# Order of four blocks in a unit of the third pass: image by image instead of column by column

## The chip, the cores and the metric

The kernel runs on one core of a Trainium2 chip. The metric is the time of one execution on the device in microseconds (us); before and after are compared by their medians over several runs. The profile is one traced execution.

## The reference: what is computed

The input x has the shape (8, 96, 96, 192), all float32. Two blocks follow each other, each of the form x + f(groupnorm(x)). The group norm has 32 groups of 6 channels, over a whole image.

The first block projects 192 channels to 384, convolves each channel by 3 x 3, runs four exponential moving averages (left, right, up and down), mixes them with the convolution, normalises over the 384 channels (layer norm) and projects back:

```python
mixed = 0.25 * (lr + rl + tb + bt) + local
mu = jnp.mean(mixed, axis=-1, keepdims=True)
var = jnp.mean(jnp.square(mixed - mu), axis=-1, keepdims=True)
normed = (mixed - mu) * jax.lax.rsqrt(var + LN_EPS) * ln_g + ln_b
return jnp.einsum('bhwc,cd->bhwd', normed, W_out) + b_out
```

The second block convolves each channel by 7 x 7, applies a layer norm, a product to 768 channels, a GELU, a product back to 192 channels and a scale per channel.

## The kernel before, in words

The kernel has five passes with DRAM arrays between them: group norm and projection (results in P_d), convolution and averages (M_d), **layer norm, projection back and the statistics of the second group norm (X1_d, X2_d)**, the 7 x 7 convolution (Y_d), and the two products with the GELU. The change lies in the third.

The third pass works through 192 **units**. A unit has two columns of pixels (WB = 2, counted by j) of two images (b = 0, 1). Every combination of column and image is a **block** of 96 pixels (S = 96, one image column) by 384 channels (C, three pieces of 128, NC = 3). The program of each engine is written out by hand, in the order of the calls (a manual schedule), so the order of the loops is the order of TensorE's queue.

- load_c(u) (lines 809 to 826) loads a unit: mt, the mixed values, 128 channels on the partitions, three transfers; and xr, the pixels of x, two transfers. It is called three units ahead; mt has four buffers.
- block_c (828 to 844) is one block. TensorE transposes the three pieces into the PSUM tile pt (L833), then multiplies them by the weights wc (L835). wc has 193 columns: 192 of the projection, and one of 1/384, so that column 192 of the result is the mean. ScalarE (ACT) copies this mean out of PSUM (L839), and then squares the transposed values minus the mean with a running sum (L842), which gives the variance.
- scale_c (846 to 851) makes 1/sqrt(variance) of the unit before, on DVE (L848) and POOL (L850).
- finish_c (853 to 874) reads the four results of the unit before from PSUM on DVE, scales them and adds xr (L858), stores them to X2_d (L867) and copies them to x1c (L871), from which store_c (L931) writes X1_d one part per unit.
- group_steps (876 to 926) are the statistics of the second group norm, spread over the units on DVE (L887, ten per unit), and at the end of each pair of images some longer steps, with small matmuls (L51, L52, L71, L911).

PSUM tiles of the results: each column has its own tile po of 128 x 2 x 193 floats, which holds both images beside each other, and there are four such tiles in all (two units). The lines that the prediction follows:

```python
831  lhs = [mt[:, m, WB - 1 - j, b, :] for m in range(NC)]
832  for m in range(NC):
833      nc.tensor.transpose(pt[:S, m * 128 : (m + 1) * 128], lhs[m], ident)
834  for m in range(NC):
835      nc.tensor.matmul(
836          po[:S, b], lhs[m], wc[:, m], start=(m == 0), stop=(m == NC - 1)
837      )
838  mean = sp.tile([S, 1], F32, tag="mean", name="mean", bufs=4)
839  nc.scalar.copy(mean, po[:S, b, D:])
...
842  nc.scalar.activation(
843      sq, pt[:S], AF.Square, bias=mean, scale=-1.0, accum_out=var[:, k : k + 1]
844  )
```

and the place that calls them, unit by unit, after the loads of three units ahead, a store, and scale_c of the unit before; the statistics' steps and finish_c of the unit before follow it:

```python
965  pos = [ps_o.tile([128, 2, D + 1], F32, tag="po", name="po") for _ in range(WB)]
966  for j in range(WB):
967      for b in range(2):
968          block_c(mt, pos[j], var, j, b)
```

The waits between engines come from the framework's tracking of tiles: a product into a po tile waits for the readers of that tile that stand before it in the program, whichever half they read.

Of the kernel before, what the change touches and what calls it, by code (L numbers as in the profile page):

```python
# [84 lines left out]
def conv_blocks_kernel(  # L85
# [137 lines left out]
    with ExitStack() as ph:  # L223
# [247 lines left out]
        with tc.manual_schedule():  # L471
# [13 lines left out]
            for b in range(B):  # L485
                more = b + 1 < B
                for t in range(n_t):
                    u = b * n_t + t

                    n, j = divmod(u - 2, NJ)  # L490
# [25 lines left out]
                    k, j = divmod(t, NJ)  # L516
# [181 lines left out]
    def load_weights():  # L698
        with nc.allow_non_contiguous_dma(reason="one value per partition"):
            for p, k, c in spans:  # L700
                nc.scalar.dma_start(w0w[p, k], w0[c])
                nc.scalar.dma_start(aff[p, k, 0:1], ln_gamma[c].unsqueeze(1))
                nc.scalar.dma_start(aff[p, k, 1:2], ln_beta[c].unsqueeze(1))
            nc.scalar.dma_start(b0g, b0.rearrange("(m p) -> p m", p=128))
        nc.scalar.dma_start(w1g, w1.rearrange("(m p) d -> p m d", p=128))
        nc.scalar.dma_start(lsc, gamma.partition_broadcast(128))
        nc.scalar.dma_start(b1g, b1.partition_broadcast(128))
# [19 lines left out]
    WB = 2  # L727
# [12 lines left out]
    def load_d(m):  # L740
        c = m * HC
        row = D * WV * B
        pool = d_pools[m % ND > 0]
        xin = pool.tile([128, NT, BP, HC, 2 * WV], F32, tag="xin", name="xin")

        for t in range(NT):
            for g, eng in enumerate((nc.sync, nc.gpsimd)):
                src = bass.AP(
                    tensor=X1_d.tensor,
                    offset=X1_d.offset + (2 * t + g) * HG * PH * row + c * WV * B,  # L750
                    ap=[[row, 64], [1, HC * WV * B]],
                )
                eng.dma_start(
                    xin[g * 64 : (g + 1) * 64, t].rearrange("q a c n -> q (a c n)"), src
                )
        band = pool.tile([128, HC, ZW], F32, tag="band", name="band1")
        for g, eng in enumerate((nc.sync, nc.gpsimd)):
            eng.dma_start(
                band[g * 64 : (g + 1) * 64].rearrange("q c l -> q (c l)"),
                Z2_d[:, c : c + HC].rearrange("r c l -> r (c l)"),  # L760
            )
        return band, xin
# [4 lines left out]
    with ExitStack() as ph:  # L767
# [41 lines left out]
        def load_c(u):  # L809

            k, v = divmod(u, n_c)
            bp, w = k // NH, v * WB * PH + k % NH
            we = w + (WB - 1) * PH + 1
            b = slice(2 * bp, 2 * bp + 2)
            mt = ip.tile([128, NC, WB, 2, S], F32, tag="mt", name="mt")
            for m in range(NC):
                nc.sync.dma_start(
                    mt[:, m].rearrange("c w b h -> c w (b h)"),
                    M_d[S - we : S - w : PH, m * 128 : (m + 1) * 128, b, :].rearrange(
                        "w c b h -> c w (b h)"  # L820
                    ),
                )
            xr = ip.tile([S, 2, WB, D], F32, tag="xr", name="xr", bufs=5)
            for i in range(2):
                nc.sync.dma_start(xr[:, i], x[2 * bp + i, :, w:we:PH, :])
            return mt, xr

        def block_c(mt, po, var, j, b):

            pt = ps_t.tile([128, C], F32, tag="pt", name="pt")  # L830
            lhs = [mt[:, m, WB - 1 - j, b, :] for m in range(NC)]
            for m in range(NC):
                nc.tensor.transpose(pt[:S, m * 128 : (m + 1) * 128], lhs[m], ident)  # L833
            for m in range(NC):
                nc.tensor.matmul(  # L835
                    po[:S, b], lhs[m], wc[:, m], start=(m == 0), stop=(m == NC - 1)
                )
            mean = sp.tile([S, 1], F32, tag="mean", name="mean", bufs=4)
            nc.scalar.copy(mean, po[:S, b, D:])  # L839
            sq = sp.tile([S, C], F32, tag="sq", name="sq", bufs=1)  # L840
            k = 2 * j + b
            nc.scalar.activation(  # L842
                sq, pt[:S], AF.Square, bias=mean, scale=-1.0, accum_out=var[:, k : k + 1]
            )

        def scale_c(var):
            ve = sp.tile([S, 2 * WB], F32, tag="ve", name="ve")
            nc.vector.tensor_scalar(ve, var, 1.0 / C, LN0_EPS * KAPPA**2, ALU.mult, ALU.add)  # L848
            rs = sp.tile([S, 2 * WB], F32, tag="rs", name="rs")
            nc.gpsimd.tensor_tensor(rs, ve, neg_half[:S, : 2 * WB], ALU.pow)  # L850
            return rs

        def finish_c(x1c, part, w, pos, rs, xr):
            x1u = sp.tile([S, WB, 2, D], F32, tag="x1u", name="x1u", bufs=3)
            for j in range(WB):
                for b in range(2):
                    k = 2 * j + b
                    nc.vector.scalar_tensor_tensor(  # L858
                        x1u[:, j, b],
                        pos[j][:S, b, :D],  # L860
                        rs[:, k : k + 1],
                        xr[:, b, j],
                        ALU.mult,
                        ALU.add,
                    )

            nc.gpsimd.dma_start(  # L867
                X2_d[part // NH, part % NH, :, w : w + WB].rearrange("h v b c -> h (v b c)"),
                x1u.rearrange("h v b c -> h (v b c)"),
            )  # L870
            nc.vector.tensor_copy(  # L871
                x1c[:, :, w : w + WB].rearrange("h c v b -> h (v b) c"),
                x1u.rearrange("h v b c -> h (v b) c"),
            )
# [53 lines left out]
        def store_c(x1c, k, q):  # L928
            c = slice(q * D // NX, (q + 1) * D // NX)
            bp, p = divmod(k, NH)  # L930
            nc.sync.dma_start(  # L931
                X1_d[p : S * PH : PH, c.start // HC : c.stop // HC, bp].rearrange(
                    "h g c v b -> h g (c v b)"
                ),
                x1c[:, c].rearrange("h (g c) v b -> h g (c v b)", c=HC),
            )
# [10 lines left out]
        with tc.manual_schedule():  # L947
            load_weights()
            for u in range(n_u + 1):
                if u + 3 < n_u:  # L950
                    ahead.append(load_c(u + 3))
                if stores:
                    stores.pop(0)()
                if held is not None:
                    rs = scale_c(held[1])
                if u < n_u:
                    mt, xr = ahead.pop(0)
                    nc.gpsimd.tensor_tensor(
                        xr.rearrange("p b w c -> p (b w) c"),
                        xr.rearrange("p b w c -> p (b w) c"),  # L960
                        cst.unsqueeze(1).to_broadcast([S, 2 * WB, D]),
                        ALU.add,
                    )
                    var = sp.tile([S, 2 * WB], F32, tag="var", name="var")
                    pos = [ps_o.tile([128, 2, D + 1], F32, tag="po", name="po") for _ in range(WB)]
                    for j in range(WB):
                        for b in range(2):
                            block_c(mt, pos[j], var, j, b)
                if steps:
                    for step in steps.pop(0):  # L970
                        step()
                if held is not None:
                    k, t = divmod(u - 1, n_c)
                    if t == 0:
                        x1c = xp.tile([S, D, WC, 2], F32, tag="x1c", name="x1c")
                    finish_c(x1c, k, t * WB, held[0], rs, held[2])
                    if (t + 1) % n_s == 0:
                        steps += group_steps(x1c, k, (t + 1) // n_s - 1)
                    if t == n_c - 1:
                        stores = [lambda q=q, x=x1c, k=k: store_c(x, k, q) for q in range(NX)]  # L980
                held = (pos, var, xr) if u < n_u else None

            stores.pop(0)()
            first_d = load_d(0)
            for store in stores:
                store()
            for step in sum(steps, []):
                step()
# [354 lines left out]
```

## Time and profile before

| what | value |
|---|---|
| median of three runs | 5908.91 us (5907.85 to 5926.22) |
| span of the profiled run | 5915.1 us |
| mean granted TensorE clock | 0.979 |
| TensorE busy | 5651.4 us, 96% |
| DVE, ACT, POOL busy | 3454.8, 2429.1, 2561.6 us |
| lines of block_c, first to last start | 1847.3 to 2928.5 us |
| products of the pass (L835) | 4608 records, 327 ns each (median) |
| copy of the mean (L839) | 768 times, 155 ns (median) |
| square with its sum (L842) | 768 times, 577 and 189 ns (median) |

How to read it: PE is TensorE's matmuls, PEld its weight loads, which run beside them. One float32 matmul stands as two records, so a block has six records of L835. A busy share is of the whole span; PE's busy time overlaps from one matmul to the next, so a PE at 100% can still be slowed by a wait. The releaser named at an idle time is the instruction that ended the wait.

### The profile page before, as it was taken

What the parts mean: (1) busy time and instruction counts of PE and PEld (TensorE: products, weight loads), DVE (VectorE), ACT (ScalarE), POOL (GpSimd) and SP (SyncE); (2) the same over time, 40 slices, a digit from 0 to 9 for tenths busy, and PEclk for the clock granted to TensorE, in tenths of its full rate; (3) what the DMA queues carried; (4) which work ended last, traced back from release to release, by engine and by line L of the source; (5) the groups of instructions that cost most, each with busy time, mean ns of one, the idle gap of its engine ahead of it and who ended that gap; (6) DMA issues with size and microseconds to landing.
All of it is one profiled execution on the core that took longest, in us unless ns stands there. A gap on an engine that the chain in (4) does not pass through costs nothing.

```text
span 5915.1 us, 122868 instructions
## 1 busy us (share of the span) xinstructions
PE 5651.4 (96%) x48550; PEld 3971.6 (67%) x48550; DVE 3454.8 (58%) x8023; ACT 2429.1 (41%) x6146; POOL 2561.6 (43%) x2731
## 2 busy tenths in 40 slices
PE   6999989999998999999878869999999999999999
PEld 3655533333335989898767757777777777777777
DVE  5555459999996667777733334444444444444443
ACT  2444447777775555555434322222222222222221
POOL 1111138888886666666522223323333333333332
PEclk9999989999999999999989989999999999999999
DMA  7999779999997889888899952232323232323221
GB/s 205 279 284 262 217 211 244 244 245 244 243 243 201 256 262 267 262 266 262 240 317 332 316 130 74 63 77 64 80 65 81 64 80 65 80 60 81 63 65 39
DMA packets 634283, 1054.49 MB, mean 178 GB/s; under 512 B 108683, under 2 KB 509284, under 8 KB 633708
## 3 DMA queue, kind: packets, MB, share of 16 engines
q1 hardware_dynamic: 516924, 620.81, 40.3%
q0 software_dynamic: 110656, 423.20, 22.0%
q8 instruction: 384, 6.29, 0.5%
q10 hardware_dynamic: 6128, 2.61, 0.2%
q14 instruction: 191, 1.56, 0.1%
HBM read 585.19 MB, written 476.72 MB: 180 GB/s over the span
## 4 chain that ended last, share of the span: by engine, by line
PE 78%; DMA 5%; issue 1%; DVE 1%; POOL 1%; SPq 0%; ACT 0%; ACTq 0%; POOLq 0%; DVEq 0%
PE po L1232 19%; PE po L835 14%; PE hp L1202 12%; PE pl L582 10%; PE hp L1212 7%; PE pa L603 5%; PE pt L833 4%; PE py L1030 3%; DMA xin<-X_d 3%; PE pa L606 2%; PE pt L1185 2%; DMA Y_d<-yo 2%; DMA X_d<-x1c 0%; DMA P_d<-po 0%; SPq L1067 0%
## 5 line engine op out<-in xcount | busy, mean ns | idle before, releaser
L1221 ACT ACTIVATE g<-hp,b0g 128x384 f32<-128x384 f32 x1152 | 564.4, 589 | 1830.5 <-PE hp L1212 1830.5
L1232 PE MATMUL po<-w1g,g 128*128 128x192 f32 x6912 | 1160.0, 327 | 0.0
L1232 PEld LDWEIGHTS po<-w1g,g 128*128 128x128 f32 x6912 | 1118.8, 190 | 1.1 <-issue 1.1
L835 PE MATMUL po<-wc,mt 128*96 128x193 f32 x4608 | 912.8, 333 | 0.0
L1189 DVE COPY yT<-pt 128x384 f32<-128x384 f32 x288 | 251.0, 871 | 1043.3 <-PE pt L1185 1043.1
L1202 PE MATMUL hp<-yT,w0w 128*128 128x384 f32 x2304 | 781.4, 489 | 0.4 <-DVE yT L1189 0.4
L835 PEld LDWEIGHTS po<-wc,mt 128*96 128x96 f32 x4608 | 701.8, 163 | 68.2 <-ACT mean L839 64.8
L1250 POOL DMA_DIRECT2D out_dram<-xo x576 | 342.9, 597 | 875.4 <-DVE xo L1239 860.6
L582 PE MATMUL pl<-pin,band 34*32 34x380 f32 (+1 forms) x13824 | 629.7, 489 | 18.5 <-DMA pin<-P_d 18.5
L1202 PEld LDWEIGHTS hp<-yT,w0w 128*128 128x128 f32 x2304 | 429.5, 191 | 257.2 <-issue 3.2
L612 DVE TENSOR_TENSOR_SCAN z<-decay,loc 128x768 f32<-128x768 f32 x288 | 505.9, 1757 | 60.1 <-ACT loc L591 30.7
L652 POOL TENSOR_TENSOR mo<-mo,z 128x768 f32<-128x768 f32 x288 | 530.1, 1841 | 3.4 <-ACT mo L607 0.4
L29 POOL TENSOR_TENSOR rs<-rs_ve,neg_half 96x8 f32<-96x8 f32 x96 | 159.2, 1659 | 824.1 <-DVE rs_ve L28 804.0
L582 PEld LDWEIGHTS pl<-pin,band 34*32 34x32 f32 x13824 | 232.7, 107 | 397.5 <-issue 396.2
L621 DVE TENSOR_TENSOR_SCAN z<-decay,z 128x768 f32<-128x768 f32 x288 | 498.3, 1730 | 0.0
L1030 PE MATMUL py<-xin,band 63*64 63x248 f32 (+1 forms) x6912 | 409.5, 392 | 74.7 <-DVE xin L1015 46.3
L842 ACT ACTIVATE sq<-pt,mean 96x384 f32<-96x384 f32 x768 | 443.5, 578 | 25.7 <-ACT mean L839 0.8
L1030 PEld LDWEIGHTS py<-xin,band 63*64 63x64 f32 x6912 | 354.4, 141 | 129.5 <-DVE xin L1015 36.5
L603 PE MATMUL pa<-loc,mix 128*32 128x384 f32 x3456 | 431.9, 493 | 0.0
L606 PE MATMUL pa<-last,down 96*32 96x384 f32 x1152 | 426.8, 493 | 1.0 <-ACT mo L607 1.0
L1212 PE MATMUL hp<-yT,w0w 64*128 64x384 f32 x2304 | 423.5, 500 | 0.0
L365 PE MATMUL pm<-xT,win 128*128 128x384 f32 x1152 | 395.8, 494 | 5.2 <-DVE po L389 5.2
(116 smaller groups left out, 7621.5 us busy)
## 6 DMA issues: line engine op xcount, KB each, us to landing
P_d<-po POOLq DMA_DIRECT2D x96, 1152.0 KB, 9.6
pin<-P_d SPq DMA_DIRECT2D x192, 576.0 KB
mt<-M_d SPq DMA_DIRECT2D x576, 192.0 KB
xq<-in_x_dram SPq DMA_DIRECT2D x96, 576.0 KB
xr<-in_x_dram SPq DMA_DIRECT2D x384, 144.0 KB
X_d<-x1u POOLq DMA_DIRECT2D x192, 288.0 KB, 4.2
X_d<-x1c SPq DMA_DIRECT2D x192, 288.0 KB
y<-Y_d SPq DMA_DIRECT2D x24, 2304.0 KB
```

The lines of the kernel that those rows point to most:

```text
L582: nc.tensor.matmul(pls[g][at * RB : (at + 1) * RB, :, lo:hi], band[rows, c, kh, :], pin[rows, c, :, NJ - 1 - j, lo + kh - 1 : hi + kh - 1] ...
L603: nc.tensor.matmul(pa[at], mix[:, i, at], loc[:, q], start=True, stop=True)
L606: nc.tensor.matmul(pa[at], down[:, to], last[:, q], start=True, stop=True)
L612: nc.vector.tensor_tensor_scan(zf, decay_f, loc.rearrange("p q n -> p (q n)"), 0.0, ALU.mult, ALU.add)
L621: nc.vector.tensor_tensor_scan(zr, decay_f, zr, 0.0, ALU.mult, ALU.add)
L652: nc.gpsimd.tensor_tensor(m, m, z, ALU.add)
L835: nc.tensor.matmul(po[:S, b], lhs[m], wc[:, m], start=(m == 0), stop=(m == NC - 1))
L1030: nc.tensor.matmul(pys[t // 2][g][k * 64 : (k + 1) * 64, t % 2, :, lo:hi], pair[k][0][rows, c, d * ZS : d * ZS + 64], pair[k][1][rows, t, ...
L1202: nc.tensor.matmul(hps[m, q], w0w[:, 2 * q, m * 128 : (m + 1) * 128], yT[:, 2 * q], start=True, stop=False,)
L1212: nc.tensor.matmul(hps[m, q], w0w[p, 1, m * 128 : (m + 1) * 128], yT[p, 1], start=False, stop=True,)
L1221: nc.scalar.activation(g[:, m, q], hps[m, q], AF.Gelu, bias=b0g[:, m : m + 1], scale=1.0)
L1232: nc.tensor.matmul(po[:, q], g[:, m, q, k * 128 : (k + 1) * 128], w1g[:, m], start=(m == 0), stop=(m == NE - 1),)
```

## The change

The two loops around block_c change places. A unit's four blocks ran in the order (column 0, image 0), (column 0, image 1), (column 1, image 0), (column 1, image 1); now both columns of one image come first and then both of the other. Products of two neighbouring blocks now go to different po tiles: the tile of column 0, of column 1, of column 0, of column 1. The change is meant to put another block between the copy of a mean out of a tile and the next products into the same tile. The places of the variances (k = 2j + b), the results and the transfers are the same.

```diff
                     pos = [ps_o.tile([128, 2, D + 1], F32, tag="po", name="po") for _ in range(WB)]
-                    for j in range(WB):
-                        for b in range(2):
+
+                    for b in range(2):
+                        for j in range(WB):
                             block_c(mt, pos[j], var, j, b)
```

## The prediction

> **What bounds the kernel now.** The order of reading was: the page's list of busy times and its 40 slices, to find the stage; the window table, to see which engine paces it; the list of waits in a stretch of it; last a timeline of one unit, to price one wait. The page first: TensorE is at the top, and one weight-load group carries an idle time put down to ScalarE's line 839.
>
> ```profile
> PE 5651.4 (96%) x48550; PEld 3971.6 (67%) x48550; DVE 3454.8 (58%) x8023; ACT 2429.1 (41%) x6146; POOL 2561.6 (43%) x2731
> L835 PEld LDWEIGHTS po<-wc,mt 128*96 128x96 f32 x4608 | 701.8, 163 | 68.2 <-ACT mean L839 64.8
> ```
>
> The lines of block_c run from 1847 to 2927 us, so the third pass takes about 1080 us, 18% of the span, for 192 units of four blocks. Four windows of 200 us in the middle of it:
>
> ```profile
> core 0: us, PE busy (x) PEld busy (x) DVE busy (x) ACT busy (x) POOL busy (x), PEclk, DMA share, GB/s
> 2000.00:2200.00 200.00, 198.88 (x1286) 179.80 (x1285) 137.72 (x462) 116.93 (x426) 133.61 (x107) 1.00 0.88 263
> 2200.00:2400.00 200.00, 200.00 (x1297) 181.48 (x1296) 144.53 (x547) 118.66 (x432) 134.95 (x108) 1.00 0.90 266
> ```
>
> The reader is to see that TensorE alone is full (200.00 of 200.00), with DVE at 72%, POOL at 67%, ACT at 59%, at the full clock, and that the DMA engines stand at 0.88 to 0.90: the second resource. A busy TensorE is not yet a TensorE at its best pace, since its spans overlap. So the waits of 2000 to 2800 us:
>
> ```profile
> ACT mean L839 <- PE po L835: 312.4, 570, 2.1
> DVE ve L848 <- ACT sq L842: 198.2, 139, 2.0
> PEld po L835 <- ACT mean L839: 48.3, 285, 0.2
> PEld gn_ps L71 <- DVE gn_ds L69: 4.3, 3, 1.5
> PEld po L835 <- DVE x1u L858: 0.5, 3, 0.2
> ```
>
> The columns are the total in us, how often, and the longest. ACT, DVE and POOL wait for TensorE or for each other, which costs nothing where TensorE paces. TensorE itself waits for ACT's copy of the mean 285 times in 143 units: two of four blocks. It never waits for a DMA here. One unit on the weight-load queue and on ACT, at 2401 to 2407 us:
>
> ```profile
> 2401.43 0.40 PEld L833 LDWEIGHTS pt<-ident,mt 128*96 128x96 f32 x3
> 2401.81 0.93 PEld L835 LDWEIGHTS po<-wc,mt 128*96 128x96 f32 x6
> 2402.75 0.40 PEld L833 LDWEIGHTS pt<-ident,mt 128*96 128x96 f32 x3
> 2403.31 0.90 PEld L835 LDWEIGHTS po<-wc,mt 128*96 128x96 f32 x6 [0.17 <-ACT mean L839]
> 2404.22 0.40 PEld L833 LDWEIGHTS pt<-ident,mt 128*96 128x96 f32 x3
> ```
>
> ```profile
> 2403.11 0.15 ACT L839 COPY mean<-po 96x1 f32<-96x1 f32 x1 [0.45 <-PE po L835]
> 2403.29 0.58 ACT L842 ACTIVATE sq<-pt,mean 96x384 f32<-96x384 f32 x1
> 2403.77 0.19 ACT L842 ACTIVATION_READ_ACCUMULATOR sq<-pt,mean 96x1 f32 x1
> ```
>
> Columns: start, duration, engine, line, what. A block is three transposes (L833) and then its products (L835). The block that begins at 2401.43 has no wait and lasts to 2402.75, 1.32 us. The next one belongs to the other image of the same column: its products go to the same po tile, the copy of the mean of the block before is still reading there (2403.11 to 2403.26), and it lasts from 2402.75 to 2404.22, 1.47 us.
>
> **What the Trainium skill says.** "PSUM — Partial Sum Buffer", section "PSUM bank collisions raise a hardware error", says that TensorE's write and another engine's read in one bank and quadrant of partitions collide even at different columns, so the guard is to be by bank and not by address. A po tile (2 x 193 floats, 1544 bytes) lies within one bank of 2 KiB by the same page's specifications. That agrees with the trace: the wait of 0.17 us stands although the copy reads column 192 of one half while the products go to the other half. "TensorE: Matmul & The Clock Gate", section "Single matmul latency", gives 166 ns plus columns/2.4 ns from the start of one warm matmul to its result; the trace has 327 ns for a record of L835 (median) against a spacing of 0.99/6 = 165 ns between records, so the result comes about 160 ns after the array has gone on. That is why the copy can't start before the transposes of the next block are well under way.
>
> **The change, part by part.** No instruction is added, removed or resized; per unit there are still 12 transposes, 12 products (24 records), four copies and four squares. Only the order differs: (column 0, image 0), (column 1, image 0), (column 0, image 1), (column 1, image 1).
>
> 1. Removed: the wait of the second block. Its products now go to the other po tile, which the copy isn't reading. What TensorE loses by one such wait is read from its matmul starts: transposes at 2401.60, 2402.91, 2404.38, 2405.69. Blocks without it take 1.31 us (2401.60 to 2402.91, 2404.38 to 2405.69), the block with it 1.47 us (2402.91 to 2404.38): 0.16 us each. Both halves of it show: products begin 0.40 instead of 0.32 us after the first transpose (2403.31 against 2401.92), and then take 1.07 instead of 0.99 us until the next transpose, since the weights of the first could not be loaded ahead. The whole pass has 383 such waits (64.8 us of idle weight-load queue). 383 x 0.16 us = 61.3 us.
>
> 2. Moved: the tiles' reuse between ACT and TensorE. The third block now writes the po tile that the copy of the first block's mean read. That copy ends about when the second block's products begin (in the timeline a copy ends at 2403.26 in the block whose products start at 2403.31), and the third block's products start a whole block, 1.31 us, later. The same holds for the fourth block and the second's copy. Slack 1.3 us against a wait of 0: I cost it at nothing, hidden by a block of matmuls.
>
> 3. Moved: the second tile of a unit is first written by the second block, not the third, so DVE must have finished reading it (L858) 1.31 us earlier. In the timeline of DVE the reads of the unit that ended at 2405.53 run from 2407.15 to 2408.52; the tile is next written in the unit that begins at 2411.09, in its second block, at about 2412.8. Slack 4.2 us: nothing. What waits behind that weight load is all of TensorE's queue, so this would be costly if it were missed; only the three units with the group norm's long steps on DVE come near. There DVE finished the four reads 0.67 us after the first block's products had begun, and the second block's begin 1.31 us after them: still in time.
>
> 4. What is given back: in those three units TensorE waits for DVE's gn_ds (L71 of the list, 1.5 us at most), and DVE's time does not shrink. TensorE arrives there 0.32 us earlier (two removed waits) and waits that much more: 3 x 0.32 = 1.0 us.
>
> 5. ACT, DVE and POOL do the same work per unit in less time. A unit now takes 5.56 us (2405.53 to 2411.09) and would take 5.24. DVE then stands at 72% x 5.56/5.24 = 76%, POOL at 71%, ACT at 62%. ACT's own block (0.15 + 0.58 + 0.19 us with small gaps, 2403.11 to 2403.96) is 0.85 us against 1.31. Nothing: TensorE hides them.
>
> 6. DMA: a unit moves 3 x 192 + 2 x 144 + 288 + 288 = 1440 KB, and the share would go from 0.89 to 0.89 x 5.56/5.24 = 0.94. Whether the queues can be packed that far the trace of before shows only indirectly: stores of x1u land 4.2 us after their issue, loads are issued three units (16 us) ahead, and no wait for a load stands in 800 us. I take 0 and keep the other end for the rivals.
>
> Sum: 61.3 - 1.0 = 60 us, all of it on the path, since TensorE paces the pass and the next pass starts behind its last unit. 5908.9 - 60 = 5849 us, a ratio of 0.990.
>
> **The rivals.** (a) DMA becomes the pace. For it: 0.89 is high, and most packets are under 2 KB. Against it: single slices of 20 us already carry 280 GB/s, and the fourth pass shows a share of 0.99 at 327 GB/s. If the mix gave no more than 270 GB/s over long, a unit would need 1440 x 1024 bytes / 270 GB/s = 5.46 us, 0.10 us less than now: 192 x 0.10 = 19 us, so 5890 us. (b) The wait comes back in another place: the third block waits for the last copy on ACT whichever tile it read, or the second waits for DVE. Against it is the slack of 1.3 and 4.2 us; for it only that the semaphore's target is not in the profile. Then 383 waits stay and the time is 5909 us. (c) Slower. A denser TensorE would be given a lower clock, or DVE's reads, now in two blocks' way, cost more than the old waits. The clock is 1.00 in this pass, and to lose the gain and 0.3% more it would have to fall by 60 + 18 = 78 us of 1018, about 8%, throughout. That gives 5927 us.
>
> **How the numbers follow.** The forecast gets 0.84, (a) 0.09, (b) 0.04, (c) 0.03. The forecast's own spread is small: the idle of 64.8 us bounds the gain from above (5844 us), and a few us of runs lie around it (the three runs of before span 5907.85 to 5926.22), so 5840 is the low end. For the high end I go half way into (a): 5876 us. Faster by over 0.3% (below 5891 us) takes the forecast and most of (a): 0.92. Within 0.3%: (b) and some of (a): 0.05. Slower: 0.03.
>
> **What would show it.** Right: the wait of L835's weight load for the mean at L839 falls from 383 times to nearly none, blocks last 1.31 us, units 5.24 us, the pass 1020 us, and the DMA share in it rises to 0.94. Step 4 right: the waits for gn_ds at L71 grow to some 1.8 us each. Wrong: waits of L833 for mt's loads in the middle of the pass would speak for (a); waits of L835 for x1u in most units, or for the mean in the third and fourth block, for (b); a clock under 1.00 in the pass for (c). A gain in this pass that is missing from the total would lie at the start of the fourth pass, in its wait for X1_d's stores.

## The result and the profile after

The changed kernel takes 5858.83 us (median of four runs, 5856.36 to 5861.74) against 5912.64 us for the kernel before, measured beside it: a ratio of 0.9905, with a 95% interval of 0.9887 to 0.9924. The forecast was 5849 us. The page's line for the weight loads of the pass, and the first two of the four windows, of the changed kernel (columns as before: busy time in the window for each engine, clock, DMA share, GB/s):

```profile
L835 PEld LDWEIGHTS po<-wc,mt 128*96 128x96 f32 x4608 | 713.1, 164 | 3.2 <-DVE x1u L858 0.5
```

```profile
2000.00:2200.00 200.00, 198.54 (x1361) 191.07 (x1360) 147.66 (x502) 123.65 (x451) 142.88 (x115) 1.00 0.94 278
2200.00:2400.00 200.00, 200.00 (x1374) 193.43 (x1373) 153.13 (x573) 125.49 (x458) 143.38 (x115) 1.00 0.96 282
```

The idle time put down to the mean is gone from the first line: 64.8 us before, none now. In the windows TensorE was full before and is full now, but it gets through 1374 matmul records in 200 us where it got through 1297, 5.9% more. This is what "busy" could not tell: the old wait lay under the tail of the matmuls in flight, whose ends the profile models, and stood only in the weight-load queue. A stretch of one unit on that queue, in the changed kernel:

```profile
2401.14 0.40 PEld L833 LDWEIGHTS pt<-ident,mt 128*96 128x96 f32 x3
2401.52 0.93 PEld L835 LDWEIGHTS po<-wc,mt 128*96 128x96 f32 x6
2402.45 0.40 PEld L833 LDWEIGHTS pt<-ident,mt 128*96 128x96 f32 x3
2402.83 0.93 PEld L835 LDWEIGHTS po<-wc,mt 128*96 128x96 f32 x6
2403.77 0.40 PEld L833 LDWEIGHTS pt<-ident,mt 128*96 128x96 f32 x3
2404.15 0.93 PEld L835 LDWEIGHTS po<-wc,mt 128*96 128x96 f32 x6
```

Blocks now last 1.31 us (2401.14 to 2402.45, 2402.45 to 2403.77), apart from those next to the small matmuls of the statistics, with 0.38 us from the first transpose's weights to the first product's; the 0.56 us of a waiting block no longer occurs. Over the pass, from the first to the last start of L835, this makes 1018 us (1849.3 to 2867.6) where it was 1077.5 us (1849.4 to 2926.9), 59 us less. Two waits of the weight-load queue for DVE, which the prediction followed, are still there from 2000 to 2800 us (total in us, how often, longest):

```profile
PEld gn_ps L71 <- DVE gn_ds L69: 5.3, 3, 1.8
PEld po L835 <- DVE x1u L858: 0.5, 3, 0.2
```

The first has grown from 4.3 us (longest 1.5) to 5.3 us (longest 1.8): TensorE arrives earlier and waits for the same DVE work. The second is as before.

The profiled runs differ by 5915.1 - 5860.0 = 55.1 us, 4 us less than the pass gained. The fourth pass took 480.6 us in the changed kernel (L1031, 2906.4 to 3387.0) against 477.4 us (L1030, 2965.7 to 3443.1), and the fifth 2390.6 against 2387.9 us. The change touches neither. The fourth, at a DMA share of about 1, took anything from 466 to 484 us in the runs below, so 3 us there can't be put down to the change.

### The profile page after: what moved, and what is told of

Its sections match the earlier page's. It is cut to its first block, busy times and chain, and to the rows that moved or that the text cites. A ratio compares the mean times of both kernels' runs of the same rounds, so it can differ in the third digit from the quotient of the medians.

```text
span 5860.0 us, 123059 instructions
## 1 busy us (share of the span) xinstructions
PE 5592.6 (95%) x48550; PEld 3974.4 (68%) x48550; DVE 3452.2 (59%) x8023; ACT 2426.3 (41%) x6146; POOL 2560.5 (44%) x2731
## 4 chain that ended last, share of the span: by engine, by line
PE 77%; DMA 6%; issue 1%; DVE 1%; SPq 1%; POOL 1%; ACT 0%; POOLq 0%; ACTq 0%; DVEq 0%
PE po L1233 19%; PE po L835 13%; PE hp L1203 13%; PE pl L582 10%; PE hp L1213 7%; PE pa L603 5%; PE pt L833 4%; DMA xin<-X_d 2%; PE pa L606 2%; PE py L1031 2%; PE pt L1186 2%; DMA Y_d<-yo 2%; DMA band<-Z_d 1%; DMA X_d<-x1c 0%; SPq L1068 0%
## 5 line engine op out<-in xcount | busy, mean ns | idle before, releaser
L835 PE MATMUL po<-wc,mt 128*96 128x193 f32 x4608 | 883.5, 327 | 0.0
L835 PEld LDWEIGHTS po<-wc,mt 128*96 128x96 f32 x4608 | 713.1, 164 | 3.2 <-DVE x1u L858 0.5
L1031 PE MATMUL py<-xin,band 63*64 63x248 f32 (+1 forms) x6912 | 406.1, 389 | 81.3 <-DVE xin L1016 50.7
L842 ACT ACTIVATE sq<-pt,mean 96x384 f32<-96x384 f32 x768 | 443.0, 577 | 25.7 <-ACT mean L839 0.8
L1031 PEld LDWEIGHTS py<-xin,band 63*64 63x64 f32 x6912 | 348.5, 140 | 138.6 <-DVE xin L1016 40.1
```

Source lines behind the costliest of these rows:

```text
L835: nc.tensor.matmul(po[:S, b], lhs[m], wc[:, m], start=(m == 0), stop=(m == NC - 1))
L1031: nc.tensor.matmul(pys[t // 2][g][k * 64 : (k + 1) * 64, t % 2, :, lo:hi], pair[k][0][rows, c, d * ZS : d * ZS + 64], pair[k][1][rows, t, ...
```

## The experiments

All were timed beside the kernel before, whose median was 5911.72 to 5913.17 us in these sessions.

**The tile or the order?** The first two runs part the two things that the change does at once. In the first the loops stay as before, and the po tile holds both columns of one image instead:

```diff
-                    po[:S, b], lhs[m], wc[:, m], start=(m == 0), stop=(m == NC - 1)
+                    po[:S, j], lhs[m], wc[:, m], start=(m == 0), stop=(m == NC - 1)
...
-            nc.scalar.copy(mean, po[:S, b, D:])
+            nc.scalar.copy(mean, po[:S, j, D:])
...
-                        pos[j][:S, b, :D],
+                        pos[b][:S, j, :D],
...
-                            block_c(mt, pos[j], var, j, b)
+                            block_c(mt, pos[b], var, j, b)
```

> Loops as before (column outside, image inside), but a po tile now holds both columns of one image instead of both images of one column, so neighbouring blocks go to different tiles. Theory (the wait is for the reader of the po tile that the next block writes): the waits of L835 for the mean vanish, blocks take 1.31 us, the pass 1019 us, the time is that of the changed kernel, 5859 us. Rival (the order of the blocks as such brings the gain, by the order in which mt or the transposes run): 383 waits stay, the pass takes 1078 us and the kernel 5912 us.

Measured: 5859.39 us, ratio 0.9915 (0.99 to 0.993), with blocks of 1.31 us and a pass of 1021.3 us from the first start of the products to their last end. All that the weight loads and the matmuls of L835 sat idle for over the whole run (us, times; here each of three waits stands on both queues):

```profile
  DVE x1u L858: 2.2, 6
```

The wait for the mean is gone. The three waits for DVE are longer than in the changed kernel (0.5 us in all), since in this layout DVE frees a unit's first tile with its third read and not with its second. The second run has the changed order with the same edit to the tiles:

> The changed order (image outside, column inside), with the po tile that holds both columns of one image: neighbouring blocks go to the same tile again. Theory: the wait comes back in the second and fourth block, 383 times 0.16 us, so 5912 us, the time of the kernel before. Rival (the order as such): 5859 us.

Measured: 5914.44 us, ratio 1.0001 (0.9994 to 1.0007). The same list of this run:

```profile
  ACT mean L839: 64.5, 383
  DVE x1u L858: 2.2, 6
```

The wait is back in full, in the order that was to be free of it, and the pass takes 1079.7 us. So the order of the blocks is nothing in itself: what counts is that two neighbouring blocks don't write the same tile. The rival that the order as such brings the gain falls in both runs. Why a whole tile is waited for isn't parted here: the framework's tracking by tile and a guard of the memory by bank would ask for the same wait, since no run lets TensorE write one half of a tile while the other is read.

**Half the dose.** The changed kernel with its last two blocks exchanged, so that one pair of neighbours in a unit shares a tile:

```diff
-                    for b in range(2):
-                        for j in range(WB):
-                            block_c(mt, pos[j], var, j, b)
+                    for j, b in ((0, 0), (1, 0), (1, 1), (0, 1)):
+                        block_c(mt, pos[j], var, j, b)
```

> The changed kernel with its last two blocks exchanged: (column 0, image 0), (column 1, image 0), (column 1, image 1), (column 0, image 1). One pair of neighbours in a unit shares a tile (second and third block). Theory: about 192 waits, one block in four at 1.47 us, the pass 1019 + 192 x 0.16 = 1049 us, the time 5859 + 31 = 5890 us. Rival (both waits must go before anything is gained, because a later wait takes up what the first gives): near 5912 us; rival (one wait costs nothing, ACT catches up): near 5859 us.

Measured: 5884.19 us, ratio 0.9953 (0.9938 to 0.9968), with this on the weight-load queue:

```profile
2400.68 0.40 PEld L833 LDWEIGHTS pt<-ident,mt 128*96 128x96 f32 x3
2401.24 0.90 PEld L835 LDWEIGHTS po<-wc,mt 128*96 128x96 f32 x6 [0.17 <-ACT mean L839]
2402.15 0.40 PEld L833 LDWEIGHTS pt<-ident,mt 128*96 128x96 f32 x3
2402.53 0.93 PEld L835 LDWEIGHTS po<-wc,mt 128*96 128x96 f32 x6
2403.46 0.40 PEld L833 LDWEIGHTS pt<-ident,mt 128*96 128x96 f32 x3
2403.84 0.93 PEld L835 LDWEIGHTS po<-wc,mt 128*96 128x96 f32 x6
2404.77 0.40 PEld L833 LDWEIGHTS pt<-ident,mt 128*96 128x96 f32 x3
2405.15 0.93 PEld L835 LDWEIGHTS po<-wc,mt 128*96 128x96 f32 x6
```

One block of four waits, 192 waits and 32.7 us of idle queue in all, 1.47 us for that block (2400.68 to 2402.15). The pass's products span 1047.6 us in this trace, from the first start to the last end, 29 us more than the 1018.7 us of the changed kernel: 0.15 us each. The medians put it at 25 us, against the 5859.39 us of the run above, where 31 us were expected. No later wait took up what the first gave, and one wait was not free: both rivals fall.

**Is it the reader's time that is lost?** The kernel before with a second copy of the mean out of the tile, which nobody reads:

```diff
             nc.scalar.copy(mean, po[:S, b, D:])
+            again = sp.tile([S, 1], F32, tag="again", name="again", bufs=4)
+            nc.scalar.copy(again, po[:S, b, D:])
```

> The kernel before with a second copy of the mean out of the po tile, into a tile that nobody reads; it stands between the copy and the square on ACT. Theory: the next products into the tile wait for the second copy too, so each of 383 waits grows by one copy and the gap to it, 0.16 to 0.19 us: 61 to 73 us more, 5973 to 5985 us. Rival (TensorE's loss is a fixed cost of a wait, not the time of the copy): the pass and the kernel stay within 10 us of before, 5912 us.

Measured: 5938.51 us, ratio 1.0044 (1.0027 to 1.0061). The sign was right, and the size about a third of what was expected: +25 us instead of 61 to 73. Blocks with a wait took 1.529 us instead of 1.470 (medians over the pass). ACT in this trace shows the term that was wrong, and the weight-load queue the wait that follows:

```profile
2401.84 0.15 ACT L839 COPY mean<-po 96x1 f32<-96x1 f32 x1 [0.46 <-PE po L835]
2401.89 0.16 ACT L841 COPY again<-po 96x1 f32<-96x1 f32 x1
2402.02 0.58 ACT L844 ACTIVATE sq<-pt,mean 96x384 f32<-96x384 f32 x1
```

```profile
2401.48 0.40 PEld L833 LDWEIGHTS pt<-ident,mt 128*96 128x96 f32 x3
2402.10 0.90 PEld L835 LDWEIGHTS po<-wc,mt 128*96 128x96 f32 x6 [0.23 <-ACT again L841]
2403.01 0.40 PEld L833 LDWEIGHTS pt<-ident,mt 128*96 128x96 f32 x3
```

The second copy starts 0.05 us after the first, not behind its end, and so ends only 0.06 us later. 383 x 0.06 = 23 us, and the pass is 23 us longer in the trace: TensorE lost just what the tile's last reader was late. So that this does not rest on so small a dose, the next run copies all 192 columns:

```diff
             nc.scalar.copy(mean, po[:S, b, D:])
+            again = sp.tile([S, D], F32, tag="again", name="again", bufs=2)
+            nc.scalar.copy(again, po[:S, b, :D])
```

> The kernel before with a wider unread copy out of the po tile on ACT, all 192 columns instead of one. From the square (384 columns, 577 ns) and the copy of one column (155 ns) it should take about 0.155 + 192 x 1.1 ns = 0.37 us, 0.21 us more than the narrow second copy, which made each wait cost 0.06 us more (blocks of 1.529 instead of 1.470 us). Theory (TensorE loses exactly what the tile's last reader is late): blocks with a wait take 1.47 + 0.06 + 0.21 = 1.74 us, 383 x 0.27 = 103 us more than before, about 6015 us. Rival (a wait has a fixed cost, and the narrow copy's effect came from something else): within 30 us of before.

Measured: 5990.77 us, ratio 1.0133 (1.0115 to 1.0151). ACT and the weight-load queue of this run:

```profile
2403.64 0.16 ACT L839 COPY mean<-po 96x1 f32<-96x1 f32 x1 [0.37 <-PE po L835]
2403.70 0.32 ACT L841 COPY again<-po 96x192 f32<-96x192 f32 x1
```

```profile
2403.28 0.39 PEld L833 LDWEIGHTS pt<-ident,mt 128*96 128x96 f32 x3
2404.07 0.90 PEld L835 LDWEIGHTS po<-wc,mt 128*96 128x96 f32 x6 [0.39 <-ACT again L841]
2404.97 0.12 PEld L833 LDWEIGHTS pt<-ident,mt 128*96 128x96 f32 x1
```

The copy took 0.32 us, not 0.37, and ends 0.22 us after the mean's (2404.02 against 2403.80). A waiting block takes 1.69 us (2403.28 to 2404.97), 0.22 us more than before: 383 x 0.22 = 84 us. The pass is 83 us longer in the trace, and the medians differ by 78 us. The expected 103 us had the copy too dear; the rule, one for one, holds at both doses. In all three traces the waiting products' weights start 0.05 us after the end of the tile's last reader: 2403.31 after 2403.26 in the kernel before, 2402.10 after 2402.05 with the narrow copy, 2404.07 after 2404.02 with the wide one.

**How much slack has the new order?** The same two edits on the changed kernel, the narrow copy first:

> The changed kernel with the second, unread copy of the mean. Theory (a whole block of 1.31 us lies between a copy and the next products into its tile): a copy more of 0.16 to 0.19 us is within the slack, ACT's block goes from 0.85 to 1.04 us, still under 1.31; no waits, 5859 us. Rival (the slack is small, or ACT's load counts): some of the 61 to 73 us that the same copy costs the kernel before.

Measured: 5858.68 us, ratio 0.9914 (0.9898 to 0.9929). Then the wide one:

> The changed kernel with the same wide unread copy. Theory: the reader still ends a good part of a block before the next products into its tile, and ACT's block of 0.85 + 0.21 = 1.06 us is under TensorE's 1.31: no wait of L835 for ACT, blocks of 1.31 us, 5859 us. Rival (the slack is shorter than half a block, or ACT's load counts): waits appear and part of the 103 us with them.

Measured: 5862.75 us, ratio 0.9913 (0.9898 to 0.9928), blocks of 1.31 us. The one wait of L835's weight loads from 2000 to 2800 us is not for ACT:

```profile
PEld po L835 <- DVE x1u L860: 0.5, 3, 0.2
```

(L860 is line 858 of the other kernels.) What costs the old order 78 us costs the new one nothing that can be measured, so ACT's longer work is not what the old order loses by. The slack can be read from the changed kernel's trace:

```profile
2402.81 0.16 ACT L839 COPY mean<-po 96x1 f32<-96x1 f32 x1 [0.46 <-PE po L835]
```

This copy reads the tile of the block that began at 2401.14 and ends at 2402.97; the next products into that tile begin at 2404.15, so the slack is 1.18 us. With the wide copy 0.96 us of it are left (median over the pass). No run came to its end.

**How near were the DMA engines?** One more load of 144 KB per unit, on the changed kernel and on the kernel before:

```diff
+            xe = ip.tile([S, WB, D], F32, tag="xe", name="xe", bufs=2)
+            nc.sync.dma_start(xe, x[2 * bp, :, w:we:PH, :])
             return mt, xr
```

> The changed kernel with one load more per unit, 144 KB of x into a tile that nobody reads: 1584 KB per unit instead of 1440 KB, which at the present 5.25 us would be 309 GB/s and a share of 1.04. If the DMA engines hold 300 GB/s in this mix (282 GB/s at a share of 0.94 to 0.96), a unit takes 1622 kB / 300 GB/s = 5.41 us: 192 x 0.16 = 31 us more, 5890 us, with waits for mt in the middle of the pass. If 282 GB/s is all they give, 5.75 us a unit: 5956 us. If the share overstates the load, 5859 us. This measures how far the DMA engines were from being the bound.

> The kernel before with the same load more per unit. At 5.56 us a unit 1622 kB are 292 GB/s. At 300 GB/s it is hidden: 5912 us. At 282 GB/s a unit takes 5.75 us: 5948 us, and then the order of the blocks would bring nothing with this load (e6 and e7 equal).

Measured: 5855.31 us, ratio 0.9909 (0.9893 to 0.9925), on the changed kernel; 5918.69 us, ratio 1.0009 (1.0002 to 1.0016), on the one before. Two windows of the first:

```profile
2000.00:2200.00 200.00, 198.56 (x1362) 191.20 (x1361) 146.37 (x497) 123.68 (x451) 141.41 (x114) 1.00 1.02 306
2200.00:2400.00 200.00, 200.00 (x1373) 193.24 (x1372) 152.44 (x570) 125.61 (x458) 142.71 (x116) 1.00 1.05 312
```

A share of 1.02 to 1.05 at 306 to 312 GB/s, the same number of matmuls as without the load to within one, and no wait of the weight loads for mt from 2000 to 2800 us. The 300 GB/s that the expectation worked out from the share was no ceiling. The load is not without a trace: the stores of x1u landed 5.6 us after their issue (median) instead of the 4.5 us of the changed kernel, and DVE now waits for stores out of x1c, which it doesn't in the changed kernel:

```profile
DVE x1c L873 <- DMA X_d<-x1c: 7.3, 3, 3.2
```

TensorE lost nothing by it. At a share of 0.94 there was room for a tenth more data; where the DMA engines would set the pace wasn't reached. The kernel before hides the load in its pass too, which takes 1078.0 us from first start to last end in the trace, against 1077.9 us; where the 7 us between its medians come from is open.

**What TensorE still loses.** Two runs were aimed at the wait for gn_ds. First only the small matmul (L71) was put one unit later, as a step of its own:

```diff
         nc.vector.tensor_reduce(ds, d, AX.X, ALU.add)
-        t["ps"] = ps = bank()
-        nc.tensor.matmul(ps[:n, 0:1], ds, avg[:, 0:1], start=True, stop=True)
+        t["ds"] = ds
+        if not split:
+            total()
+
+    def total():
+        t["ps"] = ps = bank()
+        nc.tensor.matmul(ps[:n, 0:1], t["ds"], avg[:, 0:1], start=True, stop=True)
...
+        return [means, squares, total, powers, shift], rb
```

> The changed kernel with the small matmul of the group norm's square sums (L71) as a step of its own, one unit after the DVE steps that feed it, in the third pass alone. Theory (the three waits of up to 1.8 us for gn_ds are what TensorE still loses in the pass, 5.3 us in all): they vanish, the pass takes about 1014 us instead of 1019, and the kernel 5854 us; po's wait for DVE at the same place (L858) may keep up to 1 us of each. Rival (the wait only moves to L858, since DVE ends its long steps at the same time): the pass stays at 1019 us.

Measured: 5858.15 us, ratio 0.9916 (0.9902 to 0.9931), a pass of 1019.0 us from the first start of the products to their last end, where the changed kernel has 1018.7. The expected gain did not come, and the list of waits says why:

```profile
PEld po L842 <- DVE x1u L865: 6.1, 3, 2.0
PE po L842 <- DVE x1u L865: 5.3, 3, 1.8
```

(L842 and L865 are the lines 835 and 858 of the other kernels.) The wait moved from the small matmul to the products, up to 2.0 us each: DVE reads the po tiles (L865) behind its long steps, in the order of its program, and frees them only then. The rival was right. So in the next run those steps are spread over three units, the small matmul follows a unit later, and the statistics run in 6 steps of 11 to make room:

```diff
+    def square():
+        d = t["d"]
         nc.vector.tensor_tensor(d, d, d, ALU.mult)
+
+    def reduce():
+        d = t["d"]
         nc.vector.scalar_tensor_tensor(
...
+        return [means, squares, square, reduce, total, powers, shift], rb
...
-            per = -(-len(bn) // (n_s - 1))
+            per = -(-len(bn) // (n_s - 2))
```

> The changed kernel with the group norm's long DVE steps of the third pass spread over three units (means and difference; square; sum and reduction), its small matmul a unit later, and the statistics in 6 steps of 11 instead of 7 of 10 to make room. Moving only the matmul left the wait in place, at L858. Theory (TensorE's last loss in the pass is that DVE works 6 us in one unit, so that the po tiles come free late): no step is longer than 2.5 us, both waits vanish and the pass takes about 1014 us instead of 1019, the kernel 5854 us. Rival (another wait follows): 1019 us.

Measured: 5841.19 us (5835.51 to 5846.61), ratio 0.9874 (0.9857 to 0.989). All four of its runs lie below the four of the changed kernel, though the intervals of the two ratios, each against the kernel before in its own session, still touch (0.9890 and 0.9887). In its list of waits from 2000 to 2800 us neither of the two waits for DVE is left, and its products span 1012.9 us in the pass against 1018.7 us: 5.8 us, as expected. The other 12 us between the medians of the two kernels are not explained by this: in its trace the fourth pass took 468.6 us against 480.6 us, within the 466 to 484 us that this pass took in other runs. Whether that part would stay is open.

## Why the prediction was right

- **What bounds.** That TensorE paces the pass at full clock, and that a wait in its weight-load queue counts although its busy share is full, was right: the gain is there with the wait's removal, by order or by tile, and half of it with half the waits. The copy's late start, which the prediction drew from matmul records whose ends are modelled, stands in ACT's own record too: it starts at 2403.11, 0.20 us after TensorE's next transposes (2402.91).
- **Step 1, the price of a wait.** 383 waits at 0.16 us were to give 61 us. The pass gave 59.2 us, and step 4 accounts for 1.0 of the rest. The price was read from two neighbouring blocks of one trace; the run with one wait per unit gives 0.15 us.
- **Step 2, the reuse after ACT.** At nothing, and right: no wait for the mean is left. The slack was put at 1.3 us and is 1.18, because the second block's products no longer wait for the copy and begin 0.14 us before it ends. It stood up to a reader that ends 0.22 us later.
- **Step 3, the reuse after DVE.** At nothing, and right: the same three waits for x1u, 0.5 us in all. The reading behind it was a block off. The block that begins at 2405.53 waits for the mean (at 2406.09), which a unit's first block never does; the units begin at 2404.22 and 2409.78, not at 2405.53 and 2411.09. The second tile would next be written at about 2411.5, so the slack was 3.0 us and not 4.2, still far from nothing. In the three units with long steps the reads end 0.6 us after the first block's products have begun (0.67 was said), and in the changed kernel the second block's begin 0.7 us behind them.
- **Step 4.** 1.0 us was to be given back at L71 with waits of some 1.8 us; 4.3 us became 5.3, the longest 1.8.
- **Steps 5 and 6.** DVE, POOL and ACT were to stand at 76, 71 and 62%; over the four windows they stand at 75, 71 and 62% (DVE's base of 72% was one window; the four give 71%). The DMA share was to rise to 0.94 and did. That it would cost nothing was a choice, which the trace of before could not settle; the extra load shows that there was room for a tenth more data.
- **The total.** 5849 against 5858.83 us, 10 us off. Some 4 us of this is the base: the kernel before has 5912.64 us in the comparison, not the 5908.9 us of its first three runs. One more is the pass, 59 us for 60. The other 5 us are the 59 us of the pass against the 54 us between the medians: they lie outside the pass, in the fourth and fifth by the two traces, and have no cause shown. One sum of the range was off: half way from 5849 to 5890 us is 5870 and not 5876; the measured time lies below both. Rivals (a), (b) and (c) fall: no DMA bound, no wait in another place, a clock of 1.00 in the pass.

## What to carry to other kernels

Where an engine that sets the pace writes results that another engine reads at once, look at which buffer the very next piece of work writes: if it is a neighbouring half of the same tile, the wait is here for the whole tile, and alternating the tiles removes it, by the order of the work or by what is laid into a tile. Price such a wait from two neighbouring rounds of the timeline, one with it and one without, not from the busy share, which was full in both. And look behind a wait before removing it: here one that DVE caused by its long steps moved to the next thing that DVE owed.

## What was not expected of the hardware

- Two copies on ACT that don't depend on each other overlap: the second started 0.05 us after the first though each takes 0.15 us, and 0.06 us is what it added. The square, which reads the mean, started 0.18 us after the copy with or without it.
- The share of the DMA engines stood above 1 (1.05 at 312 GB/s) with no wait of TensorE for a load: a share near 1 was no sign of a bound here.
- One and the same multiplication of the group norm on DVE (96 x 768, tile gn_d) took 2.42 to 2.43 us the three times that it met POOL's addition of the constant in the changed kernel, and 0.95 us the fourth time, when POOL did nothing. The meeting, in the kernel before, on POOL and on DVE:

```profile
2170.47 1.83 POOL L958 TENSOR_TENSOR xr<-xr,cst 96x768 f32<-96x768 f32 x1
```

```profile
2170.70 2.42 DVE L64 TENSOR_TENSOR gn_d<-gn_d 96x768 f32<-96x768 f32 x1
```

POOL ends at 2172.30, and DVE 0.82 us after that. With the long steps apart (line numbers of that run) DVE starts first, takes 0.95 us, and it is POOL's small power for the variances (L850 of the other kernels) that is drawn out, to 1.59 us instead of 1.03 (median):

```profile
2151.51 0.95 DVE L71 TENSOR_TENSOR gn_d<-gn_d 96x768 f32<-96x768 f32 x1
```

```profile
2151.76 1.59 POOL L867 TENSOR_TENSOR rs<-ve,neg_half 96x4 f32<-96x4 f32 x1 [1.87 <-DVE ve L865]
```

"SBUF — State Buffer" of the Trainium skill, section "Who interferes with whom", says that a DVE instruction with two inputs in SBUF contends with a GpSimd instruction that reads SBUF, because its second input comes through a read interface that the two share. The traces fit this: whichever starts second is late. No run was made to test it alone.
